# Fetching the rows of fourteen edge batches one by one with SyncE, their addresses loaded 32 at a time, in a graph kernel

## The chip, the core and the metric

The kernel runs on one core of a Trainium2 chip. The metric is the device time of one execution in microseconds. The core has five engines that run side by side: TensorE (PE in the profile, its weight loads PEld), VectorE (DVE), ScalarE (ACT), GpSimd (POOL) and SyncE (SP). SP does no arithmetic on data here; it starts transfers. Every time below is from one profiled execution or from the three timed runs.

## What is computed

One message-passing step over 12,500 nodes of 160 floats and 400,000 edges. The nodes are normalized, cut at zero and mapped to a table `y` (in the kernel `y_d`, in device memory). Each edge then takes the row of its source node, weighs it with numbers that a small two-layer network makes from the edge's 16 attributes, and adds it to its destination:

```python
h = jnp.maximum(_layernorm(x, axis=-1), 0.0)
y0 = x0 @ W_l1_0 * a * inv0                       # x0, x1: parts of h
y1 = jnp.einsum('nuc,uv->nvc', x1, W_l1_1) * a[:, :, None] * inv1
w = jax.nn.silu(edge_length_embedded @ fc_W1 / 4) @ fc_W2 / 8
ys0 = y0[edge_src]                                # the gather
ys1 = y1[edge_src]
mid0 = concat([w_a * ys0 * e0, w_d * einsum('euc,ec->eu', ys1, e1) / sqrt(3)])
mid1 = concat([(w_b * ys0)[:, :, None] * e1[:, None, :], (w_c * e0)[:, :, None] * ys1])
z0 = zeros.at[edge_dst].add(mid0)                 # the sum by destination; z1 likewise
out = x + C_S * (h @ W_sc) + C_X * (z @ W_l2)
```

## The kernel before

A first stage goes over the nodes in tiles of 128, writes `y_d` with transfers that ScalarE issues (L479), and lays everything else out. The main loop (L908) then goes over the edges. An edge tile is 128 edges, one to a partition; a batch is `GT` = 4 edge tiles, 782 batches in all. The order of the instructions on all five engines is the order in which they are written: nothing is rescheduled.

The 512 rows of `y_d` that a batch needs come in one of three ways. In most batches (747 of 782) GpSimd gathers them, one indirect transfer for each edge tile (`load`, L620), ten batches ahead (`AHEAD`), into eleven buffers `yg`. For 26 batches (`made_at`) the rows are computed a second time from `x` by the engines. For `BY_ROW` = 9 batches (`row_at`: batch 90 and every 78th after) SyncE fetches each of the 512 rows with a transfer of its own, 640 bytes, into one of two buffers `yr` (`rows_one_by_one`, L634). It reads the row numbers from `src_sb` into registers, four at a time (L640, an edge of each of the four tiles of one partition), then issues four transfers (L644), whose start in `y_d` is the register times 640. This work is spread evenly: at batch `b` of the loop the four-row groups are issued for which `(ahead + 1) * ROWS <= 128 * (b + 1)`, so that one batch's rows are issued over the 78 batches before it and are complete 12 batches ahead of use.

Iteration `b` of the loop writes, in this order: the re-made rows' loads, the load of the edge attributes `xe` (L311, two transfers for each eight batches, ten batches ahead, two buffers) and of the vectors `raw` (L319, once in 24 batches, two buffers), the row fetches, then on ScalarE the scaled copies `yge` (L545) and TensorE's weights `pw` (L670) for batch `b + 2`, VectorE's products (L550 to L561) for batch `b + 1`, the gather of batch `b + 10`, and TensorE's sums (L725) for batch `b`. SP thus takes `xe`, `raw` and the rows from one queue, in that order. GpSimd's gather of a batch waits for TensorE's weights of eight batches earlier.

Of the kernel before, what the change touches and what calls it, by code (L numbers as in the profile page):

```python
# [9 lines left out]
F32 = mybir.dt.float32  # L10
I32 = mybir.dt.int32
AF = mybir.ActivationFunctionType
ALU = mybir.AluOpType
# [4 lines left out]
P = 128  # L18
M0 = 64
M1 = 32  # L20
D = M0 + 3 * M1
# [3 lines left out]
ZC = 384  # L25
PC = M0 + ZC
GT = 4
# [3 lines left out]
TG = 12  # L31
EG = 8
# [5 lines left out]
HN = 2  # L38
RB = 17, 9
RS = 24, 33  # L40
FIRST_BY_ROW = 90
BY_ROW = 9
ROWS = 78
LO = D - P
EPS = 1e-5
C_S = math.sin(math.pi / 8.0)
# [4 lines left out]
def kernel(  # L51
# [19 lines left out]
    nc = tc.nc  # L71
    N = x.shape[0]
# [7 lines left out]
    while t < T:  # L80
        starts.append(t)
        n = TG
# [29 lines left out]
    y_d = dram.tile([N, D], F32, name="y_d")  # L112
# [9 lines left out]
    def made(b):  # L122

        return made_at.index(b) if b in made_at else None

    row_at = []
    while len(row_at) < BY_ROW:
        b = max(FIRST_BY_ROW, row_at[-1] + ROWS) if row_at else FIRST_BY_ROW
        while made(b) is not None:
# [28 lines left out]
    src_sb = const.tile([P, TP], I32, name="src_sb")  # L158
# [59 lines left out]
    def relate_edges(q, evp, lim):  # L218

        lo, hi = q * EG * TG, min((q + 1) * EG * TG, T)  # L220
        over = evp.tile([P, EG * TG], F32, name="over")
        up = evp.tile([P, EG * TG], F32, name="up")
        for g, k, t, n in runs_of(lo, hi):
            v = drel[:, t:t + k * n].rearrange("p (s t) -> p s t", t=n)
            o = over[:, t - lo:t - lo + k * n].rearrange("p (s t) -> p s t", t=n)
            nc.vector.tensor_tensor(o, v, lim[:, g:g + k].unsqueeze(2).to_broadcast([P, k, n]), ALU.is_ge)
            nc.vector.tensor_tensor(v, v, nbase[:, g:g + k].unsqueeze(2).to_broadcast([P, k, n]), ALU.add)
        nc.vector.tensor_reduce(fars[:, q:q + 1], over[:, :hi - lo], AX.X, ALU.max)

        nc.vector.tensor_scalar(up[:, :hi - lo], drel[:, lo:hi], float(WN), -float(WN), ALU.is_ge, ALU.mult)  # L230
        nc.vector.tensor_add(drel[:, lo:hi], drel[:, lo:hi], up[:, :hi - lo])

        nc.vector.scalar_tensor_tensor(drel[:, lo:hi], over[:, :hi - lo], float(2 * ZR), drel[:, lo:hi],
                                       op0=ALU.mult, op1=ALU.add)
# [112 lines left out]
    engines = {mybir.EngineType.PE, mybir.EngineType.Activation, mybir.EngineType.DVE}  # L347
    with (
# [140 lines left out]
        with tc.manual_schedule(engines=engines):  # L489
            for r in range(FIRST):  # L490
                c = made_at[r] * GT
# [73 lines left out]
    def implied(later, groups, reason):  # L565

        for ins in later:
            for group in groups:
                tc.declare_no_dep(ins, group=group, reason=reason)
# [6 lines left out]
    with (  # L576
# [14 lines left out]
        yrs = [yrp.tile([P, GT, D], F32, name=f"yr{i}") for i in range(min(2, len(row_at)))]  # L591
# [16 lines left out]
        def tiles_of(b):  # L608
            return list(range(first_of(b), first_of(b + 1)))

        def load(b):
            r = made(b)
            if r is not None:
                rows[b] = xms[r]
                return
            if b in row_at:
                rows[b] = yrs[row_at.index(b) % len(yrs)]
                return
            yg = rows[b] = ygs[b % YB]
            ins = [nc.gpsimd.indirect_dma_start(  # L620
                out=yg[:, k, :], out_offset=None, in_=y_d,
                in_offset=bass.IndirectOffsetOnAxis(ap=src_sb[:, t:t + 1], axis=0)).ins for k, t in enumerate(tiles_of(b))]
            if b >= AHEAD and b - AHEAD + 2 - waited[0] >= 2:
                waited[0] = b - AHEAD + 2
                tc.add_manual_dep(ins[0], weighs[waited[0]], mybir.DependencyInfo(
                    mybir.DependencyClass.Sync, mybir.DependencyReason.DATA), reason="the weights waited for the products before")
            if b >= YB:
                implied(ins, ("gathers", "lifts", "products"), "the weights waited for the last products of this buffer")
            among("gathers", issued)
            issued[:] = ins  # L630

        todo, ahead = [(i, p) for i in range(len(row_at)) for p in range(P)], [0]

        def rows_one_by_one(b):  # L634

            while todo and (ahead[0] + 1) * ROWS <= P * (b + 1):
                ahead[0] += 1
                i, p = todo.pop(0)
                c = row_at[i] * GT
                loaded = nc.values_load_multi_w_load_instructions(  # L640
                    src_sb[p:p + 1, c:c + GT], engines=[mybir.EngineType.SP], min_val=0, max_val=N - 1,
                    skip_runtime_bounds_check_because="the gathers take the same numbers")[1]
                for k in range(GT):
                    nc.sync.dma_start(yrs[i % len(yrs)][p:p + 1, k, :], y_d[ds(loaded[k], 1), :])  # L644

        def hidden(s):

# [79 lines left out]
                    leaving.append(lambda g=g: z_out(g))  # L727

        def z_out(g):
            zs = post.tile([P, ZC], F32, name="zs")  # L730
            nc.scalar.activation(zs, z_ps.pop(g), AF.Copy)
            z_sb[g] = zs

# [141 lines left out]
        with order:  # L875
            e4_load(0)
            for blk in range(min(AHEAD - 1, NB - 1) * GT // BT + 1):
                load_xe(blk)
            for b in range(min(AHEAD - 1, NB)):
                load(b)  # L880
            relate_edges(0, part, lim)
            for s in range(3):
                hidden(s)
                all_leave()
            if NQ == 1:
                any_far(next_px()[0:1, 0:1])
            for pw in pws:
                nc.vector.tensor_copy(pw[:, :, SP:], iota[:, 0:WN].rearrange("p (k c) -> p k c", k=GT))
            for b in range(min(2, NB)):
                weigh(b)  # L890
                lift_rows(b)
            dots_of(0)
            if AHEAD - 1 < NB:
                load(AHEAD - 1)
            select(0, wts[0])
            products(0)
            last_batch = [(t - 1) // GT for t in ends]
            turns_at, maps_at, adds_at = {}, {}, {}
            for g, e in enumerate(last_batch):
                at_end = e + 4 >= NB  # L900
                t = e + (1 if at_end else 2)
                m = t + 1 if at_end else min(range(t + 2, t + 8), key=lambda m: (shared.get(m, 0) + (m % 2 == 0), m))
                shared[m] = shared.get(m, 0) + 1
                turns_at.setdefault(t, []).append(g)
                maps_at.setdefault(m, []).append(g)
                a = m + (1 if at_end else 2)
                adds_at.setdefault(a + 1 if a == NB - 3 else a, []).append(g)
            for b in range(NB + 3):  # L908
                u, k = divmod(b, K)
                due(at_start, b)  # L910
                if b + AHEAD < NB:
                    load_xe((b + AHEAD) * GT // BT)
                if b < NB:
                    q, r = divmod(b, EG * K)
                    if r == 0:
                        e4_load(q + 1)
                    if r == EG * K - 8 and q + 1 < NQ:
                        relate_edges(q + 1, part, lim)
                    if r == EG * K - 4 and q + 2 == NQ:
                        any_far(next_px()[0:1, 0:1])  # L920
                rows_one_by_one(b)
                if b + 2 < NB:
                    lift_rows(b + 2)
                    weigh(b + 2)
                all_leave()
                due(on_scalar, b)
                if b + 1 < NB:
                    dots_of(b + 1)
                    if k == K - 1:
                        select(u + 1, wts[b + 1])  # L930
                    products(b + 1)
                if b + AHEAD < NB:
                    load(b + AHEAD)
                for g in adds_at.get(b, []):
                    accumulate(g)
                    leave_before(g + 1)
                due(on_vector, b)
                if b < NB:
                    sums(b)
                for g in turns_at.get(b, []):  # L940
                    turn(g)
                for g in maps_at.get(b, []):
                    map_sums(g)
                if b % 2 == 0:
                    hidden((b + 6) // 2)
                due(on_tensor, b)
# [4 lines left out]
    with (  # L951
# [10 lines left out]
        n = nc.values_load(far_i[0:1, 0:1], min_val=0, max_val=1)  # L962
        with tc.For_i(0, n, 1) as _:
# [4 lines left out]
            with tc.For_i(0, TP // GT, 1) as g:  # L968
# [34 lines left out]
                for k in range(GT):  # L1003
# [16 lines left out]
                    zs = fp.tile([P, ZC], F32, name="f_zs")  # L1020
# [63 lines left out]
```

## Time and profile before

| | |
|---|---|
| median of the three timed runs | 3892.41 us (3890.03 to 3893.6) |
| the profiled execution | 3892.34 us |
| its span, first to last instruction | 3890.6 us |
| granted TensorE clock, mean | 0.974 |
| busy: PE, DVE, POOL, ACT | 3640.6, 3478.7, 2928.2, 1897.4 us |

The difference of 1.7 us between the execution and its span lies outside the instructions. A busy share is no measure of a bound by itself: GpSimd shows 75% busy, but the idle time between two of its gathers is put down to "issue", which means that it waited for nothing that the profile shows. SP's transfers, register loads and register arithmetic aren't counted as busy; they are seen when one asks for a source line or for SP's timeline.

### The profile page before, as it was taken

Reading aid. Unit: us, or ns where it says so; the run is one execution under the profiler, and the core shown is the slowest. Engines: PE = TensorE matmul, PEld = TensorE weight load, DVE = VectorE, ACT = ScalarE, POOL = GpSimd, SP = SyncE. Lnnn points to the kernel's source line nnn. Section 1 sums busy time; section 2 is a strip of 40 time slices with the busy share of each in tenths; the row PEclk is TensorE's granted clock in tenths of the full one; section 3 lists DMA queues with packets and bytes.
Section 4 is the critical chain, followed back from the end, with each engine's and each line's share of the span. In section 5 each row is a group of like instructions: output and inputs, shape, how many; then the busy total and the mean of one; then the engine's idle time right before and its main releaser. Section 6 shows DMA issues by size and latency. Waiting matters only on the chain. (4 is left out here: it accounts for less than half of the span.)

```text
span 3890.6 us, 64721 instructions
## 1 busy us (share of the span) xinstructions
PE 3640.6 (94%) x15893; PEld 2113.5 (54%) x15893; DVE 3478.7 (89%) x6853; ACT 1897.4 (49%) x5404; POOL 2928.2 (75%) x3096
## 2 busy tenths in 40 slices
PE   6798999999999999999999999999999999999998
PEld 6454555555555555555555545555555555555555
DVE  7888889898988999999899888988999899889997
ACT  6444444444544445444544444544544445454544
POOL 7777777777777777777777777777777777777776
PEclk9899999999999999999999999999999999999999
DMA  9533333323333333333332333333333333343223
GB/s 285 149 78 78 79 79 81 80 75 78 81 79 78 81 80 75 80 79 79 78 81 75 78 78 77 79 79 78 78 78 78 79 75 81 79 126 82 74 72 88
DMA packets 236760, 337.10 MB, mean 87 GB/s; under 512 B 59195, under 2 KB 180039, under 8 KB 236119
## 3 DMA queue, kind: packets, MB, share of 16 engines
q0 software_dynamic: 148272, 253.25, 26.6%
q1 hardware_dynamic: 74434, 71.30, 6.0%
q10 hardware_dynamic: 13668, 8.36, 0.7%
q8 instruction: 126, 2.06, 0.2%
q14 instruction: 260, 2.12, 0.2%
HBM read 308.15 MB, written 24.53 MB: 86 GB/s over the span
## 5 line engine op out<-in xcount | busy, mean ns | idle before, releaser
L620 POOL DMA_INDIRECT yg<-y_d,src_sb x2985 | 2827.3, 947 | 909.8 <-issue 894.0
L725 PE MATMUL pz<-pr,sel 128*128 128x384 f32 x6250 | 2279.5, 509 | 0.0
L545 ACT ACTIVATE yge<-yg,raw 128x160 f32<-128x160 f32 x2985 | 1215.2, 425 | 1580.1 <-DMA yg<-y_d,src_sb 1563.4
L725 PEld LDWEIGHTS pz<-pr,sel 128*128 128x128 f32 x6250 | 1150.2, 194 | 828.3 <-issue 227.2
L670 PE MATMUL pw<-w,hT 64*128 64x192 f32 x6250 | 736.0, 355 | 178.0 <-DVE pr L561 176.5
L670 PEld LDWEIGHTS pw<-w,hT 64*128 64x128 f32 x6250 | 500.7, 189 | 560.8 <-DVE pr L561 307.4
L557 DVE TENSOR_TENSOR pr<-pr,pw 128x768 f32<-128x768 f32 (+1 forms) x782 | 745.0, 953 | 27.0
L550 DVE TENSOR_TENSOR tmp<-yg,pw 128x384 f32<-128x384 f32 x747 | 407.8, 546 | 259.4 <-ACT pw L672 254.9
L552 DVE TENSOR_REDUCE yg<-tmp 128x128 f32<-128x384 f32 x747 | 443.1, 593 | 26.4 <-ACT yge L545 0.7
L704 DVE TENSOR_TENSOR sel<-pw,drel 128x1536 f32<-128x1536 f32 (+1 forms) x261 | 455.0, 1743 | 0.0
L652 PE MATMUL px<-xe,w 32*128 32x512 f32 x782 | 439.1, 644 | 12.7 <-ACT hT L657 4.3
L556 DVE TENSOR_TENSOR pr<-pw,yg 128x384 f32<-128x384 f32 x747 | 413.5, 553 | 17.5
L561 DVE TENSOR_TENSOR pr<-pw,yge 128x384 f32<-128x384 f32 (+1 forms) x782 | 427.2, 546 | 0.0
L560 DVE TENSOR_TENSOR pr<-pw,yge 128x256 f32<-128x256 f32 (+1 forms) x782 | 325.2, 416 | 0.0
L672 ACT ACTIVATE pw<-raw 128x12 f32<-128x12 f32 (+1 forms) x782 | 132.8, 170 | 334.8 <-PE pw L670 333.4
L657 ACT ACTIVATE hT<-px 128x512 f32<-128x512 f32 x391 | 227.6, 582 | 2.0 <-PE px L652 1.7
L652 PEld LDWEIGHTS px<-xe,w 32*128 32x128 f32 x782 | 114.5, 183 | 196.6 <-issue 82.3
L752 PEld LDWEIGHTS px<-wc,za 128*128 128x128 f32 x720 | 97.9, 192 | 35.1 <-ACT os L757 7.1
L393 POOL DMA_INDIRECT xr<-in_x,src_sb x96 | 92.2, 961 | 29.5 <-issue 15.8
L770 DVE SCALAR_TENSOR_TENSOR acc<-os,by,acc 128x160 f32 x240 | 92.6, 386 | 18.7 <-ACT os L757 1.4
L752 PE MATMUL px<-wc,za 128*128 128x96 f32 x720 | 97.7, 272 | 6.6 <-ACT os L757 5.3
L739 PEld LDWEIGHTS pz<-ident,zs 128*128 128x128 f32 x360 | 46.9, 141 | 38.3 <-issue 21.6
(130 smaller groups left out, 1630.0 us busy)
## 6 DMA issues: line engine op xcount, KB each, us to landing
yr<-y_d SPq DMA_DIRECT2D x4608, 0.6 KB
yg<-y_d,src_sb POOLq DMA_INDIRECT x2985
xe<-in_e SPq DMA_DIRECT2D x196, 128.0 KB
xr_d<-xr SPq DMA_DIRECT2D x26, 320.5 KB
xm<-xr_d SPq DMA_DIRECT2D x26, 320.0 KB
y_d<-ys ACTq DMA_DIRECT2D x12, 640.0 KB
acc<-in_x SPq DMA_DIRECT2D x11, 640.0 KB
out<-acc SPq DMA_DIRECT2D x11, 640.0 KB
```

The costliest lines, as they stand in the source:

```text
L545: return [nc.scalar.activation(yge[:, k, :], yg[:, k, :], AF.Copy, scale=e4v[:, k, 0:1]).ins for k in range(n)]
L550: return [nc.vector.tensor_tensor(tmp[:, :n], y1, wt[:, :n, NW:NW + 3].unsqueeze(3).to_broadcast([P, n, 3, M1]), ALU.mult).ins, nc.vector. ...
L552: nc.vector.tensor_reduce(yg[:, :n, M0:96], tmp[:, :n].rearrange("p t c u -> p t u c"), AX.X, ALU.add).ins]
L556: return [nc.vector.tensor_mul(pr[:, :n, 0:96], wt[:, :n, 96:NW], yg[:, :n, 0:96]).ins, nc.vector.tensor_mul(pr[:, :n, 256:].rearrange("p ...
L557: nc.vector.tensor_mul(pr[:, :n, 256:].rearrange("p t (c u) -> p t c u", c=3), pr[:, :n, 0:M0].unsqueeze(2).to_broadcast([P, n, 3, M0]), w ...
L560: nc.vector.tensor_mul(pr[:, :n, 96:160], wt[:, :n, 0:M0], yge[:, :n, 0:M0]).ins,
L561: nc.vector.tensor_mul(pr[:, :n, 160:256].rearrange("p t (c u) -> p t c u", c=3), wt[:, :n, M0:96].unsqueeze(2).to_broadcast([P, n, 3, M1] ...
L620: ins = [nc.gpsimd.indirect_dma_start(out=yg[:, k, :], out_offset=None, in_=y_d, in_offset=bass.IndirectOffsetOnAxis(ap=src_sb[:, t:t + 1] ...
L652: nc.tensor.matmul(ph, w1[r, :], xe[r, :], start=True, stop=True)
L670: ins.append(nc.tensor.matmul(pw[:, k, 0:NW], hids[s][r, o:o + P], w2[r, :], start=True, stop=True).ins)
L704: ins = nc.vector.tensor_tensor(sels[u][:, 0:n, :].rearrange("p t (k c) -> p t k c", k=GT), for_each, drel[:, u * TG:u * TG + n].unsqueeze ...
L725: nc.tensor.matmul(z_ps[g], sels[t // TG][:, t % TG, :], pr[:, k, M0:], start=first, stop=last)
```

## The change

Fourteen batches are fetched row by row, not nine: batch 64 and every 50th after (`BY_ROW` 14, `ROWS` 50, `FIRST_BY_ROW` 64), so 7168 row transfers, not 4608, and 742 batches gathered, not 747. The row numbers of such a batch are laid into one partition of a new tile `begins` (fourteen small transfers that ScalarE issues at the start), and VectorE multiplies them once by 640, so that they are addresses in bytes. SP loads 32 of them with one instruction and issues 32 transfers from them; the table is seen as bytes, so the register is the offset. Three tiles move or lose a buffer to make room: `over`, `up`, and `zs`.

```diff
-FIRST_BY_ROW = 90
-BY_ROW = 9
-ROWS = 78
+FIRST_BY_ROW = 64
+BY_ROW = 14
+ROWS = 50
+REGS = 32
...
-        over = evp.tile([P, EG * TG], F32, name="over")
-        up = evp.tile([P, EG * TG], F32, name="up")
+        over = evp.tile([P, EG * TG], F32, name="over", bufs=1)
+        up = evp.tile([P, EG * TG], F32, name="up", bufs=1)
...
-        todo, ahead = [(i, p) for i in range(len(row_at)) for p in range(P)], [0]
+        y_bytes = y_d.rearrange("n c -> (n c)").bitcast(mybir.dt.uint8)
+        begins = yrp.tile([max(len(row_at), 1), P * GT], I32, name="begins")
+
+        def row_begins():
+
+            for i, b in enumerate(row_at):
+                nc.scalar.dma_start(begins[i:i + 1, :], src[:, b * GT:(b + 1) * GT])
+            nc.vector.tensor_scalar(begins, begins, 4 * D, None, ALU.mult)
+
+        todo, ahead, held = [(i, p, k) for i in range(len(row_at)) for p in range(P) for k in range(GT)], [0], []
 
         def rows_one_by_one(b):
 
-            while todo and (ahead[0] + 1) * ROWS <= P * (b + 1):
+            while todo and (ahead[0] + 1) * ROWS <= P * GT * (b + 1):
+                i, p, k = todo.pop(0)
+                if not held:
+                    o = p * GT + k
+                    held.extend(nc.values_load_multi_w_load_instructions(
+                        begins[i:i + 1, o:o + REGS], engines=[mybir.EngineType.SP], min_val=0, max_val=4 * D * (N - 1),
+                        skip_runtime_bounds_check_because="the gathers take the same numbers")[1])
+                nc.sync.dma_start(yrs[i % len(yrs)][p:p + 1, k, :].bitcast(mybir.dt.uint8),
+                                  y_bytes[ds(held.pop(0), 4 * D)].unsqueeze(0))
                 ahead[0] += 1
-                i, p = todo.pop(0)
-                c = row_at[i] * GT
-                loaded = nc.values_load_multi_w_load_instructions(
-                    src_sb[p:p + 1, c:c + GT], engines=[mybir.EngineType.SP], min_val=0, max_val=N - 1,
-                    skip_runtime_bounds_check_because="the gathers take the same numbers")[1]
-                for k in range(GT):
-                    nc.sync.dma_start(yrs[i % len(yrs)][p:p + 1, k, :], y_d[ds(loaded[k], 1), :])
...
         def z_out(g):
-            zs = post.tile([P, ZC], F32, name="zs")
+            zs = mr.tile([P, ZC], F32, name="zs")
...
             for b in range(min(AHEAD - 1, NB)):
                 load(b)
+            row_begins()
             relate_edges(0, part, lim)
```

How this changes SP's queue is seen early in the main loop. Of the kernel before, SP's rows for one four-row group and the start of the next (`src_sb` holds the row numbers; ISA is the arithmetic that turns a number into an address):

```order
L640 TENSOR_LOAD src_sb
L644 ISA
L644 DMA yr_1831<-y_d 1x160
L644 ISA
L644 DMA yr_1831<-y_d 1x160
L644 ISA
L644 DMA yr_1831<-y_d 1x160
L644 ISA
L644 DMA yr_1831<-y_d 1x160
L640 TENSOR_LOAD src_sb
```

Of the changed kernel, SP's rows at the same place, equal neighbours counted:

```order
L650 TENSOR_LOAD begins
L653 DMA yr_1831<-y_d 1x640 x32
L650 TENSOR_LOAD begins
L653 DMA yr_1831<-y_d 1x640 x23
L312 DMA xe<-in_e 128x1x256 x2
L653 DMA yr_1831<-y_d 1x640 x9
L650 TENSOR_LOAD begins
L653 DMA yr_1831<-y_d 1x640 x11
L320 DMA raw<-in_e 128x384
L653 DMA yr_1831<-y_d 1x640 x21
```

The arithmetic is gone, a load stands once in 32 transfers, and the loads of `xe` and `raw` stand between transfers of rows as before.

On ScalarE, at the end of the node stage, the changed kernel has this (`ys` are the last rows of the table, written by L480; L668 is the first activation of the main loop's network):

```order
L639 DMA begins<-in_src 1x128x4
L480 DMA y_d<-ys 128x8x160
L478 ACTIVATE ys<-po_135,ra 128x160
L478 ACTIVATE ys<-po_136,ra 128x160
L480 DMA y_d<-ys 128x160
L480 DMA y_d<-ys 84x160
L639 DMA begins<-in_src 1x128x4 x13
L668 ACT_TABLE_LOAD
L668 ACTIVATE hT<-px_1838 128x512
```

The rows of L639 are new; the others stood in this order before. On VectorE one row is added, the product for `begins`, just ahead of the first `over`.

## The prediction

> **What bounds the kernel now.** I read the groups by cost first, then the waits, then single engines over time.
>
> ```profile
> L620 POOL DMA_INDIRECT yg<-y_d,src_sb x2985 | 2827.3, 947 | 909.8 <-issue 894.0
> L545 ACT ACTIVATE yge<-yg,raw 128x160 f32<-128x160 f32 x2985 | 1215.2, 425 | 1580.1 <-DMA yg<-y_d,src_sb 1563.4
> ```
>
> GpSimd's gathers take 2827.3 us and the pauses between them 909.8 us, of which 894.0 us are waits for nothing: 3737.1 us for 2985 gathers, 1.252 us each. ScalarE, the first reader of the rows, spends 1563.4 us waiting for them to land. GpSimd's timeline at both ends of the main loop says that there is no hole between:
>
> ```profile
> 134.58 0.94 POOL L620 DMA_INDIRECT yg<-y_d,src_sb  x1 [0.30 <-issue]
> ...
> 3870.43 0.95 POOL L620 DMA_INDIRECT yg<-y_d,src_sb  x1 [0.30 <-issue]
> ```
>
> 3870.43 - 134.58 = 3735.85 us over 2984 steps is again 1.252 us. The other waits of the gathers are small:
>
> ```profile
>   PE pw L670: 9.2, 30
>   DMA yg<-y_d,src_sb: 4.6, 15
> ```
>
> So GpSimd never stops; every gather that goes away is worth 1.252 us, as long as nobody else becomes the last. Who could? The stretches of the main loop (busy us by engine; the last line is their sum):
>
> ```profile
> 900.00:1700.00 800.00, 760.04 (x3251) 432.48 (x3252) 727.44 (x1383) 393.35 (x1095) 605.11 (x640) 0.98 0.31 79
> ...
> sum 3740.00, PE 3541.16 PEld 2027.77 DVE 3368.74 ACT 1808.82 POOL 2829.55; mean PE 708.23 PEld 405.55 DVE 673.75 ACT 361.76 POOL 565.91
> ```
>
> TensorE has 3541.16 us of work in 3740 us, so 199 us of room, VectorE 371 us.
>
> **The change part by part.**
>
> Five batches fewer are gathered: 20 gathers x 1.252 = **25.0 us** off the path. The last batch fetched by row is 715 in both kernels and the re-made ones don't move, so what follows the last gather stays. After the change GpSimd paces the loop at 742 x 4 x 1.252 / 782 = 4.75 us a batch.
>
> The price is on SP: 2560 more transfers. What a row costs there, from SP's timeline within one group and over a longer stretch, and from the source lines:
>
> ```profile
> 1006.07 1.04 SPq L644 DMA_DIRECT2D yr<-y_d  x3
> ...
> 1005.60 24.49 SPq L644 DMA_DIRECT2D yr<-y_d  x43
> ...
> L644 SPq FUSED_REGOPS  x4608: 37/37/51, 126.5 to 3515.7; - x192
> L644 SPq MOVE yr<-y_d x4608: 29/29/38, 131.7 to 3515.7; - x192
> L644 SPq DMA_DIRECT2D yr<-y_d x4608: 224/225/323, 131.8 to 3515.8; - x192
> L640 SPq TENSOR_LOAD <-src_sb x1152: 465/563/1254, 125.2 to 3513.8; - x192
> ```
>
> Three transfers from the start of the first to the end of the last take 1.04 us, so a step is (1.04 - 0.225) / 2 = 0.408 us: 0.037 + 0.029 + 0.225, and 0.117 in three pauses. Without the arithmetic and its pause, 0.408 - 0.037 - 0.039 = 0.332 us. With loads, 43 transfers took 24.49 us; less 0.225 and 42 steps that leaves 7.13 us for ten loads, 0.71 us each: 0.15 us around a load of 0.563.
>
> A batch of the loop now has 512 / 50 = 10.24 rows: 10.24 x 0.332 = 3.40 us. The other work in SP's queue: a pair of `xe` loads in eight batches,
>
> ```profile
> 1228.55 1.16 SPq L311 DMA_DIRECT2D xe<-in_e  x2
> ...
> SPq L319 <- ACT pw L672: 369.6, 27, 22.2
> SPq L311 <- PE px L652: 306.6, 35, 41.1
> ...
> SPq L644 <- DMA xe<-in_e: 8.4, 26, 0.6
> ```
>
> 1.16 us each. Every transfer waits for the one eight places earlier to land; the 26 waits of up to 0.6 us show that `xe` lands some 4.7 us after its issue (1.16 us, and six rows at 24.49 / 43 = 0.57), while six rows will take only 2.0 us. I add 2 us a pair: 3.16 / 8 = 0.40 us a batch. Some 75 other transfers (`raw`, `xm`, stores) of at most 0.6 us are 0.06 us a batch. Together 3.86 us of 4.75; 0.89 us is left for 0.32 loads, so **a load of 32 may take 0.89 / 0.32 - 0.15 = 2.6 us**. Below that SP still waits for buffers, as it does for 676 us now (the two long waits above), and its work is hidden under GpSimd's. Each microsecond above it costs 224 loads x 1 us.
>
> No row shows a load of 32. Rows that bound it (the number loaded is one in all of these):
>
> ```profile
> L764 DVEq TENSOR_LOAD <-tile_i x120: 298/304/553, 295.0 to 3880.5; - x120
> L962 POOLq TENSOR_LOAD <-far_i x1: 490/490/490, 3863.1 to 3863.1; - x1
> L962 PEldq TENSOR_LOAD <-far_i x1: 483/483/483, 3880.7 to 3880.7; - x1
> ```
>
> From below: nothing for a register, 0.56 us. By GpSimd's and TensorE's single loads: (563 - 485) / 3 = 26 ns a register, 563 + 28 x 26 = 1.3 us. By VectorE's: (563 - 304) / 3 = 86 ns, 563 + 28 x 86 = 3.0 us. From above: all of SP's 563 ns in proportion, 141 ns each, 4.5 us. I take 1.3 us: two of the three kinds of single load cost nearly what SP's four do, and even half way to the 3.0, at 2.1 us, the result is the same. With 1.3 us SP needs 3.86 + 0.32 x 1.45 = 4.32 us of 4.75.
>
> The Trainium skill speaks on both sides of this. "DMA: Bandwidth & Descriptors", "Latency and other measured facts", gives a load into registers a floor of about 600 ns that unrolling shares out, which is near the 563 measured and would leave 32 almost free. "Runtime: NRT & Kernel Launch", "Instruction fetch mechanics", gives some 200 ns for each register even in bulk, which four registers in 563 ns contradict here; by it a load would be 6.4 us and the kernel near 4690 us.
>
> The start: ScalarE issues fourteen loads more. One stands ahead of a write of `y_d`, 0.6 us at the price of an `xe` load. The table was whole when SP's first row left, at 131.8 (above), 2.8 us before the first gather, which covers it. Thirteen stand ahead of ScalarE's first activation, 13 x 0.58 = 7.5 us:
>
> ```profile
> 140.82 1.28 ACT L657 ACT_TABLE_LOAD   x1 [16.09 <-DMA yg<-y_d,src_sb]
> 140.89 0.27 DVE L226 TENSOR_TENSOR over<-drel,lim 128x96 f32<-128x96 f32 x1 [2.73 <-DMA yg<-y_d,src_sb]
> ```
>
> ScalarE waits there for 16.09 us, and VectorE, which must wait for the fourteen to land before its product and `over`, until 140.89 anyway. Zero; uncovered it would be up to 10 us at the loop's start, and the loop has ten batches of gathers in hand to take that up. The single buffers cost nothing: `over` and `up` are written and read by VectorE alone, and a `zs` is turned two batches after it is made, with the next at least three batches behind it. The new places of the row batches lead by 14 batches, not 12.
>
> Sum: 3892.34 - 25.0 = **3867.3 us** against the profiled execution, which is the median of the runs to 0.1 us.
>
> **The rivals.**
>
> SP becomes the bound, because registers are read one after another at VectorE's price. The place is the queue that holds `xe` behind the rows: `xe` is issued ten batches and needed six batches ahead, so SP may be only four batches late, some 19 us; then TensorE's weights wait, and the gathers for them. A load of 3.0 us is 0.4 above the limit: 224 x 0.4 = 90 us, less the 25 or so that SP may be late and early, gives 3867 + 65 = 3932 us. For it: 3 x 86 added to 304 is SP's 563 exactly. Against it: the 483 and 490. The point from which it decides is 2.6 us.
>
> The same at the full proportion, 4.5 us: 224 x 1.9 - 25 = 400 us, 4268 us. Against it: even the single loads have a part that doesn't depend on the number. The page with 200 ns a register would be beyond this.
>
> TensorE takes over. Its 3541 us of work now stand in 3715 us. If half of the gain were eaten by stalls in front of it, 3880 us. For it: 95% busy in every stretch. Against it: after each spared batch ScalarE stops waiting for rows, and the profile shows those waits come back, so the readers do catch up:
>
> ```profile
> ACT yge L545 <- DMA yg<-y_d,src_sb: 5.4, 6, 1.8
> ...
> ACT yge L545 <- DMA yg<-y_d,src_sb: 1.8, 2, 1.1
> ```
>
> (21 us before the use of batch 90 and 21 us after it.)
>
> The change doesn't do what it says: a transfer of bytes is cut into more pieces than one of floats and costs SP more than 0.332 us. From 0.42 us a row (with 1.3 us loads) SP decides, and the time passes 3892 soon after. Nothing in the trace speaks for it; the order shows one transfer a row.
>
> **How the numbers follow.** Forecast 0.60; SP bound with loads near 3 us 0.22; full proportion 0.05; TensorE takes part of the gain 0.08; dearer transfers, or something at the start, 0.05. About 0.2% (8 us) is what a measurement of this kernel tells from no change. Faster: 0.60 and half of the fourth and a little of the SP case, 0.65. Same 0.05, slower 0.30. The forecast's own range is 3863 to 3874 us. To leave out no more than 2 in 10 the range must reach the 3932 us of the first rival: 3862 to 3940.
>
> **What would show it.** Right: 2965 gathers, still 1.25 us apart without a hole, the last near 3845; SP's waits for `xe` and `raw` buffers shorter than 676 us but there; row transfers 0.33 us apart; loads of 32 under 2.6 us. Wrong: SP's waits for buffers gone, GpSimd's waits for `pw` in tens of microseconds, TensorE's `px` waiting for `xe`; then the load's duration says which rival it is.

## The result, and the profile after

The changed kernel takes 3872.11 us (median of five runs, 3870.65 to 3872.75) against 3892.41 us: a ratio of 0.9946 with a 95% interval of 0.9935 to 0.9958 (the two medians alone give 0.9948). That is 20.3 us less, where 25.0 were forecast. The execution that was profiled took 3870.65 us, with a span of 3868.6 us. The kernel before ran again beside each group of experiments, at 3900 and 3897 us and, in one group at granted clocks of 0.80 to 0.86, at 5309 us, so each time below is read against the kernel before of its own group, and of the last group only the durations of single instructions.

The gathers of the changed kernel, from its page and from GpSimd's timeline (start, duration, both in us; then line, operation and the idle time before):

```profile
L621 POOL DMA_INDIRECT yg<-y_d,src_sb x2965 | 2807.0, 947 | 904.2 <-issue 882.6
```

```profile
134.85 0.94 POOL L621 DMA_INDIRECT yg<-y_d,src_sb  x1 [0.30 <-issue]
...
3844.84 0.95 POOL L621 DMA_INDIRECT yg<-y_d,src_sb  x1 [0.30 <-issue]
```

There are twenty fewer, still 3709.99 / 2964 = 1.252 us apart without a hole. The first starts 0.27 us later than before, the last 25.59 us earlier. The readers follow: the last two sums on VectorE start at 3882.14 us before the change (first line, VectorE's timeline of the kernel before) and at 3856.33 us after it (second line, of the changed kernel), 25.8 us earlier.

```profile
3882.14 0.81 DVE L770 SCALAR_TENSOR_TENSOR acc<-os,by,acc 128x160 f32 x2 [1.03 <-ACT os L757]
```

```profile
3856.33 0.80 DVE L781 SCALAR_TENSOR_TENSOR acc<-os,by,acc 128x160 f32 x2 [1.01 <-ACT os L768]
```

So the main loop gave the whole of what was forecast. What is missing is lost behind it: from the end of the last sum to the end of the span the kernel before takes 3890.6 - 3882.95 = 7.6 us, the changed one 3868.6 - 3857.13 = 11.4 us (from unrounded times). The drains of the program's end on GpSimd and on SP, by source line, of the kernel before and of the changed one (count, shortest/median/longest in ns, first and last start):

```profile
L1080 POOLq DRAIN  x3: 45/103/1290, 3885.3 to 3890.3; - x3
L1080 SPq DRAIN  x3: 7/7/13, 3889.7 to 3890.0; - x3
```

```profile
L1092 POOLq DRAIN  x3: 45/103/8313, 3859.4 to 3868.3; - x3
L1092 SPq DRAIN  x3: 7/7/13, 3863.5 to 3868.0; - x3
```

A drain is an instruction that stands at the program's end on every engine, ahead of the last barrier. GpSimd's first drain here lasts 8.31 us instead of 1.29. Of these 7.0 us only 3.8 lengthen the kernel: before the change GpSimd's drain ended at 3886.6 us and SP came last to the barrier at the end, at 3889.7; after it SP is there at 3863.5 us and the engines wait until GpSimd's drain ends, at 3867.8. Of the profiled 21.7 us (3892.34 to 3870.65), 25.8 are the loop and -3.8 this end; the 1.4 us between 21.7 and the 20.3 of the medians lie within the scatter of the five runs.

SP, by source line of the changed kernel, its waits while it has rows to issue (us in total, times, longest), and four rows in its timeline:

```profile
L650 SPq TENSOR_LOAD <-begins x224: 2040/2150/2411, 145.3 to 3473.2; - x112
L653 SPq DMA_DIRECT2D yr<-y_d x7168: 224/225/1042, 147.6 to 3486.0; - x200
```

```profile
SPq L653 <- DMA xe<-in_e: 154.9, 140, 2.2
SPq L320 <- ACT pw L683: 102.3, 19, 13.1
SPq L320 <- ACT zs L742: 24.0, 5, 9.1
SPq L345 <- DVE tmp L551: 20.5, 1, 20.5
SPq L312 <- PE pw L681: 9.1, 17, 0.9
```

```profile
176.52 1.19 SPq L653 DMA_DIRECT2D yr<-y_d  x4
```

A load of 32 registers takes 2.15 us, a row (1.19 - 0.225) / 3 = 0.32 us. The waits for another engine, most of them for a buffer that it must free (the last four of the five lines), are 156 us in 3340: SP is within 5% of being the bound. That is the number that the experiments test.

At the start ScalarE and VectorE are later than before:

```profile
127.59 15.27 ACTq L639 DMA_DIRECT2D begins<-in_src  x13
143.20 1.28 ACT L668 ACT_TABLE_LOAD   x1 [17.35 <-DMA yg<-y_d,src_sb]
```

```profile
144.70 0.41 DVE L640 TENSOR_SCALAR begins<-begins 14x512 int32<-14x512 int32 x1 [6.27 <-DMA begins<-in_src]
```

The table load starts at 143.20 and not 140.82, 2.4 us later; the gathers don't notice.

### The profile page after: what moved, and what is told of

It is laid out like the page before. It is cut to its first block, busy times and chain, and to the rows that moved or that the text cites. A ratio compares the mean times of both kernels' runs of the same rounds, so it can differ in the third digit from the quotient of the medians.

```text
span 3868.6 us, 64351 instructions
## 1 busy us (share of the span) xinstructions
PE 3627.7 (94%) x15893; PEld 2108.3 (54%) x15893; DVE 3476.5 (90%) x6854; ACT 1882.1 (49%) x5404; POOL 2907.8 (75%) x3076
## 5 line engine op out<-in xcount | busy, mean ns | idle before, releaser
L546 ACT ACTIVATE yge<-yg,raw 128x160 f32<-128x160 f32 x2965 | 1193.3, 425 | 1486.7 <-DMA yg<-y_d,src_sb 1475.1
L668 ACT ACTIVATE hT<-px 128x512 f32<-128x512 f32 x391 | 227.6, 582 | 2.0 <-PE px L663 1.7
```

The lines of the kernel that those rows point to most:

```text
L546: return [nc.scalar.activation(yge[:, k, :], yg[:, k, :], AF.Copy, scale=e4v[:, k, 0:1]).ins for k in range(n)]
```

## The experiments

Two theories stand at the outset. The first, that of the prediction: GpSimd's gathers set the pace, a spared batch is worth five microseconds, SP's work is hidden until it exceeds GpSimd's. The rival: SP (or TensorE) already takes part, and the missing five microseconds are its doing. A third question is the drain.

### The addressing alone, and twelve batches

```diff
-FIRST_BY_ROW, BY_ROW, ROWS = 64, 14, 50
+FIRST_BY_ROW, BY_ROW, ROWS = 90, 9, 78      # e1_nine
+FIRST_BY_ROW, BY_ROW, ROWS = 72, 12, 58     # e5_twelve
```

> The new addressing alone: nine batches as before (first 90, every 78th), addresses in bytes, 32 to a load. If GpSimd's gathers set the time, the 2985 gathers are back and the time is that of the kernel before, 3892 us within 2, although SP's rows cost 0.32 us and not 0.41 and its waits for buffers grow. If the cheaper addressing or the moved buffers bring part of the gain by themselves, it is 3885 or less. If what is lost behind the last gather (GpSimd's final drain, 8.3 us after the change, 1.3 us before) hangs on how many instructions GpSimd has, the drain is 1.3 us again here.

Measured: 3900.0 us beside 3900.05 for the kernel before, a ratio of 1.000 (0.999 to 1.001). The cheaper addressing, the single buffers and the additional work at the start are worth nothing by themselves.

> Twelve batches by row (first 72, every 58th). If each batch less to gather is worth four gathers of 1.252 us, this is two batches dearer than fourteen: 3872 + 10 = 3882 us. If SP or TensorE already ate part of the gain at fourteen, twelve is no worse than 3877.

Measured: 3890.36 us beside 3900.05, ratio 0.9976 (0.9966 to 0.9985). The steps between kernels of this group: nine to twelve batches -9.6 us, twelve to fourteen (the kernel with twenty memsets below, 3878.7) -11.7 us. Three batches should be worth 15.0 us, two 10.0. The differences are again the final drain, 1.29 us with nine batches (first line below), 8.97 with twelve (second line) and 8.31 with fourteen:

```profile
L1092 POOLq DRAIN  x3: 45/103/1290, 3893.2 to 3897.5; - x3
```

```profile
L1092 POOLq DRAIN  x3: 45/103/8967, 3878.4 to 3888.2; - x3
```

Behind the last sum the profiles show 7.3 us with nine, 12.6 with twelve and 11.3 with the memsets: -15.0 + 5.3 = -9.7, and -10.0 - 1.3 = -11.3. So each batch gave its five microseconds.

### One batch more

```diff
-FIRST_BY_ROW, BY_ROW, ROWS = 64, 14, 50
+FIRST_BY_ROW, BY_ROW, ROWS = 60, 15, 46     # e4_fifteen
```

> Fifteen batches by row (first 60, every 46th), all else as changed. In the changed kernel SP waits about 156 us for buffers while it has rows to issue. A batch more costs it 512 x 0.32 us and 16 loads x 2.3 us, 201 us. By that sum SP is 45 us short, of which some 20 are covered by what it may be late: 3867 + 25 = 3892 us, with GpSimd waiting for TensorE's weights. If SP has more room than its waits show, GpSimd still sets the pace: 3872 - 5 = 3867 us.

Measured: 3925.26 us beside 3900.05, ratio 1.0064 (1.0047 to 1.0081): 25 us longer than with nine batches. Against fourteen in the same group (3878.7 us) it should have gained 5 us and lost 46.6, so 51.6 us are lost. GpSimd's waits before its gathers (us, times), and one of TensorE's (us, times, longest):

```profile
  issue: 881.7, 2889
  PE pw L681: 63.5, 51
```

```profile
PE px L663 <- DMA xe<-in_e: 71.8, 33, 4.8
```

GpSimd now stops for TensorE's weights, some 48 us beyond the usual 0.30 us before each of these 51 gathers, and TensorE stops for `xe`, a wait that the changed kernel's trace doesn't have. While SP has rows to issue (the last leaves at 3515.7 us) it waits for other engines only some 7 us, not 156. This is the first rival of the prediction, one batch further on.

The sum of the expectation had SP 45 us short. It left out that with `ROWS` 46 the rows are issued in 15 x 46 = 690 batches and not 14 x 50 = 700, which takes ten batches, 47 us, from SP's time: 201 + 47 - 156 = 92 us short. The leave, what SP may be late before anyone waits, was there. In the changed kernel SP issues a pair of `xe` loads some 38 us before TensorE's first use of it (median over the middle of the loop); with fifteen batches that falls from 29 us near the start to some 6 us and stays there until the rows end. So about 25 to 30 us are covered, and 92 less these is 62 to 67 us, not far above the 51.6 measured.

### What a row and a load cost SP

```diff
-REGS = 32
+REGS = 16        # e3_regs16, e10_regs16
+REGS = 4         # e2_regs4, e11_regs4
```

> Sixteen to a load. If the price of a load rises evenly from 0.563 us for four to 2.15 for 32 (57 ns each), it is 1.24 us for sixteen; SP has 108 us more work, its waits of 156 us cover that, and the time stays 3872. If a load has one price above some number, 2.15 us, SP has 515 us more work and the time is about 4200.

> The kernel with sixteen to a load once more, on an undisturbed chip. The price of the load is 1.23 us by the run before, on the even line from 0.56 (four) to 2.15 (32). SP has 448 x 1.23 - 224 x 2.15 + 224 x 0.15 = 103 us more to do than with 32, against 156 us of waits for buffers: time as with 32, within 4 us of it. If the waits that the profile shows are not room, as the run with fifteen batches suggests (33 us later than its sum), it is 10 to 60 us slower than that.

> Fourteen batches, addresses in bytes, but four to a load. By the SP budget a row costs 0.32 + 0.71 / 4 = 0.50 us, a batch of the loop 10.24 x 0.50 + 0.40 = 5.5 us against GpSimd's 4.75: SP is the bound over some 700 batches, 3867 + 700 x 0.75 - 25 = about 4370 us. If SP's work is hidden whatever it is, 3872.

> The kernel with four to a load once more, on an undisturbed chip: SP has 1792 x 0.71 - 224 x 2.30 = 757 us more to do, less 156 us of waits: about 600 us slower, 4470 us. If hidden, 3872.

The kernel with sixteen took 5502.78 us beside 5308.97, with loads of 1.23 us, and 3871.0 us beside 3897.38, with these loads:

```profile
L650 SPq TENSOR_LOAD <-begins x448: 1135/1247/1526, 144.3 to 3479.3; - x150
```

With four to a load (5812.56 us beside 5308.97, and 4304.2 beside 3897.38) a load takes 0.558 us. 0.56, 1.25, 2.15 for 4, 16, 32: 57 ns for each register more. The 3871.0 and the 4304.2 us are one run each. Sixteen to a load keeps the time of 32: the last gather starts at 3844.8 us in both profiles, and SP's waits for other engines while it has rows fall from 156 to 66 us, so some 90 us more of its work were hidden. Four to a load gives 433 us more than sixteen, a smaller loss than the 600 expected. The last row leaves at 3944.9 us and not 3486.0:

```profile
L653 SPq DMA_DIRECT2D yr<-y_d x7168: 224/228/714, 144.8 to 3944.9; - x200
```

459 us more, and the waits for other engines, 156 us, all but used up, and the waits for `xe` halved (79.2 us for 154.9): some 690 us of additional work, where the sum had 757. The loads themselves are 1792 x 0.558 - 224 x 2.15 = 518. Around a load stand not the 0.15 us that the sums used but 0.07: from one row's start to the next the trace shows 0.95 us in the median with a load of four between and 0.32 without. For 1568 loads more that is some 110 us; the remaining 60 or so are not traced to an instruction. The kernel becomes 433 us longer while the last row is 459 us late: the difference of 25 us is the leave again.

```diff
-            nc.vector.tensor_scalar(begins, begins, 4 * D, None, ALU.mult)
+            nc.vector.tensor_scalar(begins, begins, 1, None, ALU.mult)
...
-                nc.sync.dma_start(... , y_bytes[ds(held.pop(0), 4 * D)].unsqueeze(0))
+                nc.sync.dma_start(... , y_d[ds(held.pop(0), 1), :])          # e8_scaled, e12_scaled
```

> Row numbers in the one partition, 32 to a load, but SP multiplies each by the row's size itself, as before the change. The step is 0.40 us again, 10.24 x 0.076 = 0.78 us a batch more, 545 us in all against 156 us of waits and some 20 of leave: 3872 + 370 = about 4240 us. If the arithmetic is hidden behind the issue of the transfer before, 3872.

> The kernel that multiplies on SP, 32 to a load, once more, on an undisturbed chip: 7168 x 0.076 = 545 us more on SP, less 156 us: about 390 us slower, 4260 us. If the arithmetic is hidden behind the issue of the transfer before, 3872.

Measured: 6321.52 us beside 5308.97, and 4265.33 us beside 3897.38 (one run each), the latter 394 us more than with sixteen to a load and without the arithmetic. Four rows in SP's timeline of this second run, to set beside the four of the changed kernel:

```profile
1002.11 1.44 SPq L653 DMA_DIRECT2D yr<-y_d  x4
```

A row costs (1.44 - 1.19) / 3 = 0.083 us more than without the arithmetic. So an instruction of 37 ns, with its pause, stands in SP's way in full; nothing hides it. Over 7168 rows that is some 600 us, not 545. About 150 us of it go into waits for other engines and 46 into shorter waits for `xe` (108.6 us for 154.9), and the last row leaves at 3905.4 us, 419 us later than in the changed kernel; 25 us of that are leave. That 545 - 156 comes within 5 us of the measured 394 is luck: the step was taken too small, and two of these terms were left out. GpSimd's waits show where the lateness arrives:

```profile
  issue: 858.0, 2812
  PE pw L680: 419.9, 130
```

So both parts of the cheaper addressing are needed for fourteen batches: without the addresses in bytes, or with loads of four, the same fourteen batches make the kernel some 10% slower than before.

### The drain

```diff
                 due(on_tensor, b)
+            for _ in range(20):                  # e6_pad20; 84 in e7_pad84
+                nc.gpsimd.memset(pad, 0.0)
```

> The changed kernel with twenty tiny memsets on GpSimd behind its last gather, so that it has as many instructions as before the change. They lie in GpSimd's idle time behind the gathers. If the 8.3 us of the final drain come from where GpSimd's last instructions stand in its stream, the drain is 1.3 us again and the time falls by about 4 us, to 3868. If the drain waits for something of SP's or of the transfers, it stays 8 us and the time 3872.

> As the run with twenty memsets, but 84 of them. If GpSimd's final drain hangs on where its last instructions stand in the stream, it changes again, to some value between 1 and 9 us, and the time with it by at most 5 us. If it is a matter of time or of transfers, it is as in the changed kernel, 8.3 us.

Measured: 3878.7 us, ratio 0.9946 (0.9929 to 0.9963), the same ratio as the changed kernel; with 84 memsets 5434.68 us beside 5308.97. The drains of the two:

```profile
L1096 POOLq DRAIN  x3: 45/103/8313, 3867.8 to 3876.6; - x3
```

```profile
L1096 POOLq DRAIN  x3: 45/103/8313, 5429.0 to 5437.9; - x3
```

8313 ns to the nanosecond, whatever the number of GpSimd's instructions and the pace: this guess fell. What the drain does go with is the number of gathers: 8967, 8313 and 7987 ns with 2973, 2965 and 2961 of them, 82 ns for each (the 7987 is from the kernel with fifteen batches). With 2985 it is 1290 ns, both before the change and with nine batches in the new addressing, so the line does not go on to there; what happens between 2973 and 2985, the runs don't show. In all these kernels SP's rows grow by 512 whenever the gathers fall by four, so by these durations alone the drain could go with the rows as well.

```diff
                 due(on_tensor, b)
+            nc.gpsimd.drain()                    # e9_drain
```

> The changed kernel with a drain of GpSimd written right behind its last gather, where it has some 12 us of nothing to do. The final drain took 1.29 us with 2985 gathers, 8.97, 8.31 and 7.99 us with 2973, 2965 and 2961, whatever else GpSimd had to do: 82 ns for each gather, so it looks like work left over from the gathers. If so, the early drain takes the 8.3 us, hidden, the final one is short, and the time behind the last sum falls from 11.4 us to about 7.6: 3868 us where the changed kernel takes 3872, a ratio of 0.9936 to the kernel before. If the drain waits for something at the end itself, the final one stays 8.3 us and the ratio 0.9946.

Measured: 3873.57 us beside 3897.38, ratio 0.9939 (0.9925 to 0.9953). GpSimd's early drain and those at the end, by source line:

```profile
L960 POOLq DRAIN  x1: 16713/16713/16713, 3842.5 to 3842.5; - x1
```

```profile
L1094 POOLq DRAIN  x3: 39/41/103, 3865.2 to 3870.1; - x3
```

The record of the early drain begins while gathers are still ahead of it; it ends at 3859.2 us, 8.3 us after the last gather's end (3850.9), and the first of the final ones then takes 41 ns. Behind the last sum 7.5 us are left, as before the change. In the changed kernel the drain starts 13.6 us after the last gather's end (3845.8) and takes the same 8.3 us, and with 84 memsets 45 us after it. So the first drain behind the gathers takes this time whenever it comes; it does not run off by itself while GpSimd is idle, but a drain placed in that idle time takes it off the end. The gain of 3.9 us is seen in this end alone: in the timed runs the interval overlaps that of the changed kernel, so whether this version is faster than the changed one isn't settled.

## Why the prediction was right, and where it was not

**What bounds the kernel: right.** Twenty gathers less moved the last sums forward by 25.8 us, and 9, 12, 14 batches lie on the same line once the end is taken apart. TensorE, which was 95% busy, took nothing; that rival falls.

**"What follows the last gather stays": wrong.** This is the step that failed, and it cost 3.8 of the 25.0 us. I read the program's end as a constant because the same instructions stand in it. One of them, GpSimd's drain, has a duration that changes with the number of batches gathered, and the profile of before shows only its shortest case, 1.29 us. Why it is short there stays open.

**The price of a row: right within 4%.** 0.332 forecast; 0.32 measured in the four rows above, and 0.33 in the mean over all rows, waits left out. That the arithmetic and its pause come off the path in full is shown by the run that puts them back, where a row costs 0.083 us more. The limit of 0.42 us a row that the prediction names for dearer transfers leaves out the loads that it says it includes: (4.75 - 0.46 - 0.32 x 1.45) / 10.24 is 0.37.

**The price of a load: mis-sized, without consequence.** I took 1.3 us from GpSimd's and TensorE's single loads; it is 2.15, near the half way (2.1) that I named as still harmless. That it stayed under the limit was in part luck, since the bounds of 1.3 and 3.0 lay on both sides of it. SP's own slope is 57 ns a register, between the 26 and the 86 of the bounds; single loads on other engines were no measure for either end. The view from which the prediction took 490 and 483 ns has three more single loads, of 909 ns (VectorE), 1073 ns (ScalarE) and, on SP itself:

```profile
L962 SPq TENSOR_LOAD <-far_i x1: 1531/1531/1531, 3802.8 to 3802.8; - x1
```

Single loads scatter from 0.30 to 1.53 us; only loads of several numbers on SP could give the slope. The Trainium skill's two figures ("DMA: Bandwidth & Descriptors", "Latency and other measured facts", a floor of about 600 ns; "Runtime: NRT & Kernel Launch", "Instruction fetch mechanics", some 200 ns a register, beside loads that the runtime injects) don't hold for these loads: four registers in 0.56 us lie near the floor, but VectorE's single ones of 0.30 us lie below it, and the price rises with the count, at 57 ns and not 200 in these runs.

**The limit of SP: right, and close.** I had 2.6 us as the longest harmless load. The measured 156 us of room over 224 loads put it at 2.15 + 0.7 = 2.85 us. The difference is what stands around a load, 0.07 us and not 0.15, and the waits for `xe`, 154.9 us over the 87 pairs that fall among the rows, 1.8 us each and not 2; with these the prediction's own sum gives 0.93 / 0.32 - 0.07 = 2.8 us. The 676 us of waits that the prediction starts from are those of the whole kernel; between SP's first row and its last the same two waits of the kernel before are 328.6 + 124.2 = 453 us. The first rival, SP as the bound with TensorE waiting for `xe` and GpSimd for the weights, is what happens with fifteen batches, with loads of four and with the arithmetic, by the mechanism named, and with the leave of 25 us or so that the prediction gave SP.

**The start: right that it costs nothing, wrong in what it takes.** The thirteen loads hold ScalarE's queue for 15.3 us, not 7.5, and VectorE waits 6.3 us for them. The first products come 2.4 us later; the gathers in hand absorb it, as the equal times of nine batches show. SP's first row leaves at 147.6 us and not at 131.8, so 16 us of SP's time go there, and the 156 us are what is left after them.

## What to carry to other kernels

When one engine issues without a hole, count what it issues: its number times its step is the gain, and it came here to within a microsecond. What is laid on another engine's queue has its own limit, found by adding up every instruction and pause in that queue per step of the bounding engine, then checking the sum against that queue's waits for other engines: here 156 us of waits meant that one more batch was too many. The time in which the queue must be done belongs in the sum as well; left out, it made the forecast of that run's loss half of what was measured. And look at the ends separately: here a change in the number of transfers changed how long the last drain takes.

## What was not expected of the hardware

GpSimd's final drain took 1.29, 7.99, 8.31 or 8.97 us with 2985, 2961, 2965 or 2973 gathers (82 ns a gather from 2961 to 2973, and short at 2985), and neither memsets nor loads nor the pace changed it; it is as long 45 us after the last gather as right behind it. A load into SP's registers rose by 57 ns for each number: 0.56, 1.25, 2.15 us for 4, 16, 32. And a gather's step differed by 2 to 3 ns between executions, 1.252 us in the profiles of the kernel before and the changed one and 1.254 to 1.255 with nine and twelve batches, which over 3000 gathers is some 8 us.
